# A transformer with local attention on one Trainium2 core: one of four rotations per tile moved ahead of its squares, and the sum of those squares moved behind the first average

## The chip, the cores and the metric

The kernel runs on one core of a Trainium2 chip. The metric is the device time of one execution in microseconds; lower is better. A core has five engines that work beside each other, each through its own list of instructions in order: TensorE (PE; its weight loads are shown as PEld), VectorE (DVE), ScalarE (ACT), GpSimd (POOL) and SyncE (SP, which issues transfers). An instruction starts when the one ahead of it on its engine lets it and the semaphores that it waits for have been raised.

## The reference

The model is a chain of four blocks on x of shape (4, 512, 128); each block is a cross attention to a context of 77 rows and then a feed-forward part, which is a mixture of 8 experts in blocks 0 and 3, and a quantised network with a depthwise convolution in block 1. In block 2 it is a local transformer of six layers, and the change lies there:

```python
def attn_layer(x, Wqkv, qs, ksc, Wo):
    qkv = x @ Wqkv
    q, k, v = split into 16 heads of 64
    q = l2norm(q) * qs
    k = l2norm(k) * ksc
    q = q * cos * scale + rotate_half(q) * sin * scale
    k = k * cos / scale + rotate_half(k) * sin / scale
    out = local_attention(q, k, v)      # windows of 32, each sees itself and the one before
    return out @ Wo
for i in range(6):
    x = attn_layer(shift_tokens(x), ...) + x
    x = ffn_layer(shift_tokens(x), ...) + x    # layernorm, W1, a * gelu(gate), W2
```

`l2norm` divides each head's 64 numbers by the root of the sum of their squares. That sum is what the change moves.

## The kernel before, in words

All other blocks are scheduled by a planner (`Plan`); the local transformer is not. In `local_transformer` the order of the work is written out by hand in one loop (L2027), under a manual schedule: every engine gets its instructions in the order in which the loop's body names them.

The activations stay on the chip: `Y[b]` holds a sequence of 512 tokens, features on partitions. The work is cut into tiles of 128 tokens: 6 layers x 4 sequences x 4 tiles = 96. One pass of the loop (a slot) works on three tiles at once: tile T is projected, rotated and normalised; tile T1, one behind, has its queries and keys turned to features on partitions and its scores and softmax computed; tile T2, two behind, has its averages, its output projection and its residual. Beside them a feed-forward F of one sequence runs over four slots, called phases 0 to 3 (n - 6 modulo 4): layernorm moments, norm and turning in phase 0, gate in 1 and 2, up in 2 and 3, down in 3. So 90 of the 96 slots with a tile T have one phase of a feed-forward too.

The steps that the change and the prediction touch:

- `queries_or_keys(T, kind, c)` (L1767): one matmul (L1774, it runs as two passes) gives 512 columns, that is 8 heads, of queries (kind 0) or keys (kind 1), c = 0 or 1, into `ps_mm`, a ring of two PSUM banks; ScalarE squares them into `sq` (L1776), a ring of two buffers.
- `rotate(T, kind, c)` (L1779): VectorE multiplies the bank by a table into `rc` (L1784, ring of six), then the halves swapped by another table into `rs` (L1787, ring of two), then sums `sq` over each head into `ss` (L1796); GpSimd adds `rs` to `rc` (L1797).
- `normalise(T)` (L1800): once all four sums are there, VectorE (L1807, L1808) and GpSimd (L1812 to L1815) find the inverse roots and GpSimd scales the four `rc` (L1818).
- `probabilities(T2)` (L1901): TensorE transposes P (L582), ScalarE copies it to `PT` in two halves (L1904).
- `average(T2, g)` and `normalised(T2, g)` (L1906, L1921): 64 small matmuls (L1914) into the bank pair `av`, then VectorE's reciprocal (L1923) and product (L1924).
- `scores(T1)` and `softmax(T1)` (L1866, L1889): the scores go into a bank pair `sc`, of which there is one; VectorE takes the maximum (L1893) and subtracts it into `P` (L1894); ScalarE's exponential follows (L1899).
- `ff_stage`: its matmuls (L1951, L1961, L1972, L1983, L1995) take the same pair `sc`; VectorE's part is L510 to L522 and L1711 in phase 0 and L1986 in phase 3; GpSimd finds a root (L514, L515) between L512 and L522.

On VectorE a slot reads, in order: first rotation of queries with its sum, [statistics in phase 0, or a product of the feed-forward in phase 3], reciprocal and product of the first average, [norm in phase 0], second rotation with its sum, reciprocal and product of the second average, two rotations of keys with their sums, L1807, L1808, maximum, subtraction, residual (L1945).

The ring of two in PSUM means that the third projection of a tile can start only when the bank of the first has been read by both ScalarE and VectorE. The framework makes the second reader of a bank wait for the first one: before the change, L1784 waits for L1776.

Of the kernel before, what the change touches and what calls it, by code (L numbers as in the profile page):

```python
# [25 lines left out]
ALU = mybir.AluOpType  # L26
AX = mybir.AxisListType
# [94 lines left out]
def bc(ap, shape, *axes):  # L122

    for a in axes:
        ap = ap.unsqueeze(a)
    return ap.to_broadcast(shape)
# [112 lines left out]
def tile_kernel(ctx: ExitStack, tc: tile.TileContext, A: dict, out: bass.AP):  # L239
    nc = tc.nc  # L240
    V, G, SC, PE, DMA = nc.vector, nc.gpsimd, nc.scalar, nc.tensor, nc.sync
# [40 lines left out]
    def p_mm(*shape):  # L282
        return psum(shape, "mm", 2)

    def p_tr(*shape):
        return psum(shape, "tr", 2)
# [54 lines left out]
    for b in range(B):  # L341
        t = xpool.tile([128, NT, D], F32, name=f"x{b}", tag=f"x{b}")
# [26 lines left out]
    with banks(), tc.tile_pool(name="prep", bufs=1) as prep:  # L369
# [26 lines left out]
        t = p_tr(128, B, SK)  # L396
# [3 lines left out]
        t = p_tr(128, 4, D)  # L400
# [3 lines left out]
        t = p_tr(128, 8)  # L404
# [3 lines left out]
        t = p_tr(128, 2, E)  # L408
# [1281 lines left out]
    def local_transformer(Y):  # L1690
        with ExitStack() as es:
# [28 lines left out]
            def load(i):  # L1720


                W = A["L2_ffn_Wqkv"][i]
                w = []
                for j in range(4):
                    t = wp.tile([128, 512], F32, name="wqk", bufs=8)
                    DMA.dma_start(t, W[:, 512 * j : 512 * j + 512])
                    w.append(t)
                wv = wp.tile([128, 2, 512], F32, name="wv")
                for x0 in range(2):  # L1730
                    DMA.dma_start(
                        wv[:, x0].rearrange("p (k d) -> p k d", d=LD),
                        W[:, 2 * INNER :].rearrange("p (k x d) -> p x k d", x=2, d=LD)[:, x0],
                    )
                wo = wp.tile([128, 8, D], F32, name="wo")
                DMA.dma_start(wo, A["L2_ffn_Wo"][i].rearrange("(c p) d -> p c d", p=128))
                w1 = wp.tile([128, 2 * DI], F32, name="lw1")
                DMA.dma_start(w1, A["L2_ffn_W1"][i])
                w2 = wp.tile([128, 3, D], F32, name="lw2")
                DMA.dma_start(  # L1740
                    w2[:, 0:2], A["L2_ffn_W2"][i][0:256].rearrange("(c p) d -> p c d", p=128)
                )
                DMA.dma_start(w2[: CH_W[2], 2], A["L2_ffn_W2"][i][256:DI])
                qs = wp.tile([128, 2, LD], F32, name="qs")
                DMA.dma_start(qs[:, 0], A["L2_ffn_q_scale"][i].partition_broadcast(128))
                DMA.dma_start(qs[:, 1], A["L2_ffn_k_scale"][i].partition_broadcast(128))
                return w, wv, wo, w1, w2, qs
# [19 lines left out]
            def queries_or_keys(T, kind, c):  # L1767

                b, tt = T.b, T.tt
                if T.ss is None:  # L1770
                    T.ss = small.tile([128, 2, LH], F32, name="ss")
                lhs = Y[b][:, 128 * tt : 128 * tt + 128]
                t = p_mm(128, 8, LD)
                PE.matmul(t, lhs, T.w[2 * kind + c], start=True, stop=True)  # L1774
                sq = tp.tile([128, 8, LD], F32, name="sq")
                SC.activation(sq, t, AF.Square)  # L1776
                T.raw[kind, c] = t, sq

            def rotate(T, kind, c):  # L1779

                tt = T.tt
                t, sq = T.raw.pop((kind, c))
                a = tp.tile([128, 8, LD], F32, name="rc", bufs=6)
                V.tensor_tensor(a, t, bc(T.tabs[:, 2 * kind, tt], [128, 8, LD], 1), ALU.mult)  # L1784

                r = tp.tile([128, 8, LD], F32, name="rs")
                V.tensor_tensor(  # L1787
                    r.rearrange("p h (x d) -> p h x d", x=2),
                    t.rearrange("p h (x d) -> p h x d", x=2)[:, :, ::-1],
                    bc(  # L1790
                        T.tabs[:, 2 * kind + 1, tt].rearrange("p (x d) -> p x d", x=2),
                        [128, 8, 2, LD // 2], 1,
                    ),
                    ALU.mult,
                )
                V.tensor_reduce(T.ss[:, kind, 8 * c : 8 * c + 8], sq, AX.X, ALU.add)  # L1796
                G.tensor_tensor(a, a, r, ALU.add)  # L1797
                T.rot[kind, c] = a

            def normalise(T):  # L1800


                n = 2 * LH
                ss = T.ss.rearrange("p a b -> p (a b)")
                y = small.tile([128, n], F32, name="rn_y")
                t = small.tile([128, n], F32, name="rn_t")
                V.tensor_scalar(ss, ss, 1e-24, -0.5, ALU.max, ALU.mult)  # L1807
                V.tensor_scalar(  # L1808
                    y.bitcast(I32), ss.bitcast(I32), -0.5, 0x5F3759DF - 0x40400000, ALU.mult, ALU.add
                )  # L1810
                for _ in range(3):
                    G.tensor_tensor(t, y, y, ALU.mult)  # L1812
                    G.tensor_tensor(t, t, ss, ALU.mult)
                    G.tensor_scalar(t, t, 1.5, None, ALU.add)
                    G.tensor_tensor(y, y, t, ALU.mult)  # L1815
                for (kind, c), a in sorted(T.rot.items()):
                    o = LH * kind + 8 * c
                    G.tensor_tensor(a, a, bc(y[:, o : o + 8], [128, 8, LD], 2), ALU.mult)  # L1818
# [135 lines left out]
            def ff_norm(F):  # L1954
                F.xn = lnp.tile([128, NT, D], F32, name="xn")
                layernorm(F.xn, F.t, F.found)
# [70 lines left out]
            for n in range(len(tiles) + 10):  # L2027
                T = tiles[n] if n < len(tiles) else None
                T1 = tiles[n - 1] if 0 <= n - 1 < len(tiles) else None
                T2 = tiles[n - 2] if 0 <= n - 2 < len(tiles) else None  # L2030
                m, phase = divmod(n - 6, 4)
                F = rows[m] if 0 <= m < len(rows) else None
                if T:
                    if n % 16 == 7 and T.i + 1 < DEPTH:
                        loaded[T.i + 1] = load(T.i + 1)
                    if n == 4:
                        fill, send, send_back = clear(lnp, 1)
                        fill(G)
                        send(DMA)
                        send_back(DMA)  # L2040
                    if n % 16 == 15 and T.i + 1 < DEPTH:
                        tabs[T.i + 1] = tables(loaded[T.i + 1][5])
                    T.before = tiles[n - 1] if T.tt else None
                    T.w, T.wv, T.wo = loaded[T.i][:3]
                    T.tabs = tabs[T.i]
                    queries_or_keys(T, 0, 0)
                if T2:
                    probabilities(T2)
                if T:
                    queries_or_keys(T, 0, 1)  # L2050
                    rotate(T, 0, 0)
                if F:
                    ff_stage(F, phase, False)
                if T2:
                    average(T2, 0)
                if T1:
                    turned(T1, 0)
                if T:
                    queries_or_keys(T, 1, 0)
                if T2:  # L2060
                    normalised(T2, 0)
                if F and phase == 0:
                    ff_norm(F)
                if T:
                    rotate(T, 0, 1)
                if T2:
                    average(T2, 1)
                if T1:
                    turned(T1, 1)
                if T:  # L2070
                    queries_or_keys(T, 1, 1)
                if T2:
                    normalised(T2, 1)
                if T:
                    rotate(T, 1, 0)
                if T2:
                    attended(T2)
                if T and T.tt == NT - 1 and n + 1 < len(tiles):
                    swap(tiles[n + 1].b)
                if T1:  # L2080
                    scores(T1)
                if T:
                    rotate(T, 1, 1)
                if T:
                    normalise(T)
                if T1:
                    softmax(T1)
                if T2:
                    project_out(T2)
                    residual(T2)  # L2090
                if T:
                    values(T, 0)
                    values(T, 1)
                if F:
                    ff_stage(F, phase, True)

            for b in range(B):
                for r, o in ((slice(0, 64), 0), (slice(64, 128), 1)):
                    t = p_tr(128, NT, 64)
# [38 lines left out]
```

## Time and profile before

| | |
|---|---|
| median of three runs | 2546.58 us (2539.14 to 2553.28) |
| the profiled execution | 2546.81 us, of which 2545.0 us span |
| granted TensorE clock, mean | 0.955 |
| busy: TensorE, VectorE, ScalarE, GpSimd | 89%, 70%, 48%, 60% of the span |
| busy in 1000 to 1400 us, inside the local transformer | TensorE 379.46, VectorE 322.16, ScalarE 222.35, GpSimd 302.30 of 400 us |
| first and last projection of the local transformer (L1774) | 519.2 and 2213.5 us |
| VectorE's softmax subtraction (L1894) | 96 times, 1.225 us each |

The local transformer is two thirds of the span. Its slots repeat so closely that one can lay them on top of each other: from one subtraction L1894 to the next it is at the median 20.15 us in a phase 0 slot, 15.65 in phase 1, 17.54 in phase 2 and 17.12 in phase 3, each taken from end to end. A row of a timeline has the start of an instruction, its duration, its engine and line, what it writes and reads, and in brackets how long its engine was idle before it and what ended that. A duration on VectorE is longer than the distance to the next start, since the end of one instruction overlaps the start of the next: two rotations that follow each other take 0.68 us each and start 0.60 us apart.

### The profile page before, as it was taken

The page shows a single profiled execution, that of the slowest core. Times are in us where ns is not written, and L with a number is a line of the kernel's source. Part 1 is how long each engine was busy: PE and PEld are TensorE (multiplying, and loading weights), DVE is VectorE, ACT ScalarE, POOL GpSimd, SP SyncE. Part 2 cuts the span into 40 slices and gives each one's busy share as a digit, 9 for nine tenths or more (in the row PEclk, how much of TensorE's full clock was granted, in tenths as well). Part 3 has the DMA queues.
Part 4 walks back from the last instruction along what each step waited for, and adds up shares of the span by engine and source line. Part 5 has one row for each costly group of instructions (what it writes and reads, how often), then busy time and mean ns, then how long its engine had stood idle before and what let it go on. Part 6 is the DMA issues. An engine that isn't in the chain of part 4 may idle for free.

```text
span 2545.0 us, 87636 instructions
## 1 busy us (share of the span) xinstructions
PE 2275.1 (89%) x37341; PEld 1472.7 (58%) x37341; DVE 1792.1 (70%) x4016; ACT 1228.5 (48%) x2161; POOL 1538.1 (60%) x2613
## 2 busy tenths in 40 slices
PE   7969799968999999999999999999999999978776
PEld 3547444536666666666666666666666666644455
DVE  5543475757787787878778787887878778737522
ACT  3622144534555555555555555555555555514322
POOL 2333303367777777777777777777777777702543
PEclk9979789989999999999999999999999999978888
DMA  6201200026211120101201121111211111011023
GB/s 165 81 27 39 67 1 2 1 58 138 72 30 34 28 77 26 34 26 34 77 25 34 28 76 34 26 32 28 77 31 29 34 28 34 26 36 49 27 67 89
DMA packets 134304, 116.20 MB, mean 46 GB/s; under 512 B 29505, under 2 KB 102700, under 8 KB 133916
## 3 DMA queue, kind: packets, MB, share of 16 engines
q1 hardware_dynamic: 128373, 102.81, 15.5%
q0 software_dynamic: 4608, 7.35, 0.9%
q8 instruction: 296, 4.85, 0.8%
q14 instruction: 92, 0.75, 0.1%
q10 hardware_dynamic: 935, 0.43, 0.1%
HBM read 42.84 MB, written 21.52 MB: 25 GB/s over the span
## 4 chain that ended last, share of the span: by engine, by line
PE 48%; DVE 31%; issue 6%; ACT 6%; POOL 6%; DMA 2%; SPq 0%; ACTq 0%; POOLq 0%; DVEq 0%
PE ps_mm L1774 6%; PE ps_tr L582 6%; DVE rc L1784 5%; DVE rs L1787 5%; DVE ss L1796 5%; PE ps_av L1938 3%; PE ps_sc L1983 3%; PE ps_tr L1853 3%; PE ps_av L1914 3%; PE ps_sc L1995 3%; DVE P L1894 2%; PE ps_sc L1883 2%; DVE la_mx L1893 2%; DVE ss L1807 2%; PE ps L1312 2%
## 5 line engine op out<-in xcount | busy, mean ns | idle before, releaser
L1797 POOL TENSOR_TENSOR rc<-rc,rs 128x512 f32<-128x512 f32 x384 | 488.2, 1273 | 281.8 <-DVE rs L1787 256.9
L1774 PE MATMUL ps_mm<-wqk,y 128*128 128x512 f32 x768 | 400.1, 604 | 35.3 <-DVE rs L1787 32.1
L1784 DVE TENSOR_TENSOR rc<-ps_mm,tabs 128x512 f32<-128x512 f32 x384 | 262.5, 684 | 204.0 <-ACT sq L1776 189.1
L1818 POOL TENSOR_TENSOR rc<-rc,rn_y 128x512 f32<-128x512 f32 x384 | 388.3, 1042 | 7.5
L1776 ACT ACTIVATE sq<-ps_mm 128x512 f32<-128x512 f32 x384 | 231.8, 604 | 177.1 <-PE ps_mm L1774 134.9
L1899 ACT ACTIVATE P<-P 128x1024 f32<-128x1024 f32 x96 | 101.5, 1057 | 435.5 <-DVE P L1894 435.5
L1787 DVE TENSOR_TENSOR rs<-ps_mm,tabs 128x512 f32<-128x512 f32 x384 | 261.6, 681 | 5.0 <-POOL rc L1797 4.7
L1796 DVE TENSOR_REDUCE ss<-sq 128x8 f32<-128x512 f32 x384 | 259.6, 676 | 0.0
L1914 PEld LDWEIGHTS ps_av<-v,PT 64*32 64x32 f32 x12288 | 140.5, 105 | 139.2 <-PE ps_tr L582 71.6
L582 PE MATMUL ps_tr<-cst,rc 128*128 128x128 f32 x1536 | 211.5, 281 | 9.8 <-POOL rc L1818 5.7
L1938 PE MATMUL ps_av<-aT,wo 128*128 128x128 f32 x1536 | 198.3, 282 | 3.5 <-issue 3.4
L1938 PEld LDWEIGHTS ps_av<-aT,wo 128*128 128x128 f32 x1536 | 179.2, 191 | 13.2 <-issue 4.6
L582 PEld LDWEIGHTS ps_tr<-cst,rc 128*128 128x128 f32 x1536 | 166.0, 141 | 29.6 <-POOL rc L1818 6.8
L1914 PE MATMUL ps_av<-v,PT 64*32 64x65 f32 x12288 | 172.6, 225 | 4.4 <-DVE attn L1924 1.1
L1774 PEld LDWEIGHTS ps_mm<-wqk,y 128*128 128x128 f32 x768 | 122.9, 193 | 80.1 <-DVE rs L1787 41.1
L1883 PE MATMUL ps_sc<-kT,qT 64*32 64x64 f32 x12288 | 145.8, 225 | 25.2 <-issue 18.4
L1017 POOL DMA_INDIRECT back<-ye,to x80 | 77.4, 968 | 141.8 <-DVE ye L1131 102.2
L1883 PEld LDWEIGHTS ps_sc<-kT,qT 64*32 64x32 f32 x12288 | 140.3, 105 | 34.9 <-issue 21.5
L1830 ACT COPY qT<-ps_tr 128x512 f32<-128x512 f32 x192 | 103.2, 589 | 91.7 <-PE ps_tr L582 89.4
L763 ACT ACTIVATE P<-ps,deltaT 77x512 f32<-77x512 f32 x192 | 115.0, 682 | 63.3 <-PE ps L757 63.2
L1830 ACT COPY kT<-ps_tr 128x512 f32<-128x512 f32 x192 | 103.2, 589 | 81.3 <-PE ps_tr L582 80.0
L1924 DVE TENSOR_TENSOR attn<-ps_av,la_den 128x512 f32<-128x512 f32 x192 | 132.8, 691 | 6.6
(391 smaller groups left out, 4449.4 us busy)
## 6 DMA issues: line engine op xcount, KB each, us to landing
v<-v SPq DMA_DIRECT2D x432, 65.0 KB
v<-v SPq DMA_DIRECT2D x96, 195.0 KB
wqk<-in_L_ffn_Wqkv_dram SPq DMA_DIRECT2D x24, 256.0 KB
sent<-xn SPq DMA_DIRECT2D x2, 2210.0 KB
xe<-sent SPq DMA_DIRECT2D x16, 260.0 KB
back<-xn SPq DMA_DIRECT2D x2, 2048.0 KB
raw<-in_L_ffn_W_dram SPq DMA_DIRECT2D x8, 512.0 KB
yb<-back SPq DMA_DIRECT2D x16, 256.0 KB
```

The source lines that it names most:

```text
L582: PE.transpose(t[:, i], src[:, i], ident)
L1774: PE.matmul(t, lhs, T.w[2 * kind + c], start=True, stop=True)
L1776: SC.activation(sq, t, AF.Square)
L1784: V.tensor_tensor(a, t, bc(T.tabs[:, 2 * kind, tt], [128, 8, LD], 1), ALU.mult)
L1787: V.tensor_tensor(r.rearrange("p h (x d) -> p h x d", x=2), t.rearrange("p h (x d) -> p h x d", x=2)[:, :, ::-1], bc(T.tabs[:, 2 * kind + ...
L1796: V.tensor_reduce(T.ss[:, kind, 8 * c : 8 * c + 8], sq, AX.X, ALU.add)
L1797: G.tensor_tensor(a, a, r, ALU.add)
L1818: G.tensor_tensor(a, a, bc(y[:, o : o + 8], [128, 8, LD], 2), ALU.mult)
L1830: SC.copy(t[:, 4 * c : 4 * c + 4, lead:], to_features(T.rot[kind, c].rearrange("p (k x) d -> p k (x d)", x=2)),)
L1883: PE.matmul(T.banks[32 * w : 32 * w + 32, z, k], T.qT[r, k, 32 * w : 32 * w + 32], T.kT[r, k, 32 * w : 32 * w + 64], start=False, stop=Tru ...
L1914: PE.matmul(T.means[32 * w : 32 * w + 32, x0, k], T.PT[r, 4 * g + k, 32 * w : 32 * w + 32], (T.v1 if w % 2 else T.v2)[r, x0, 4 * g + k], s ...
L1938: PE.matmul(t, T.wo[:, c], T.aT[:, c], start=(c == 0), stop=(c == 7))
```

## The change

The square of the first half of the queries (kind 0, c 0) is taken out of `queries_or_keys`, and its sum out of `rotate`. In the slot, the first rotation now comes ahead of that square and right behind the first projection's matmul and the copies of P's transposes; the second projection follows. The sum comes behind the reciprocal and product of the first average (in phase 0 behind the norm too), just ahead of the second rotation. So VectorE is the first reader of that bank, and ScalarE waits for it. The other three quarters of a tile keep their order.

```diff
                 PE.matmul(t, lhs, T.w[2 * kind + c], start=True, stop=True)
+                T.raw[kind, c] = [t, None]
+                if kind or c:
+                    squares(T, kind, c)
+
+            def squares(T, kind, c):
+                t = T.raw[kind, c][0]
                 sq = tp.tile([128, 8, LD], F32, name="sq")
                 SC.activation(sq, t, AF.Square)
-                T.raw[kind, c] = t, sq
+                T.raw[kind, c][1] = sq
 
             def rotate(T, kind, c):
...
-                V.tensor_reduce(T.ss[:, kind, 8 * c : 8 * c + 8], sq, AX.X, ALU.add)
                 G.tensor_tensor(a, a, r, ALU.add)
                 T.rot[kind, c] = a
+                if kind or c:
+                    summed(T, kind, c)
+
+            def summed(T, kind, c):
+                sq = T.raw.pop((kind, c))[1]
+                V.tensor_reduce(T.ss[:, kind, 8 * c : 8 * c + 8], sq, AX.X, ALU.add)
...
                 if T2:
                     probabilities(T2)
                 if T:
+                    rotate(T, 0, 0)
+                    squares(T, 0, 0)
                     queries_or_keys(T, 0, 1)
-                    rotate(T, 0, 0)
                 if F:
                     ff_stage(F, phase, False)
...
                 if F and phase == 0:
                     ff_norm(F)
                 if T:
+                    summed(T, 0, 0)
                     rotate(T, 0, 1)
```

In the changed kernel L1776, L1784, L1787, L1796, L1894, L1914, L1923 and L1986 are L1782, L1790, L1793, L1809, L1905, L1925, L1934 and L1997.

More of the change, by code (lines that the diff above doesn't have):

```diff
@@ L1774, in queries_or_keys @@
                 PE.matmul(t, lhs, T.w[2 * kind + c], start=True, stop=True)
+                T.raw[kind, c] = [t, None]
[3 more added lines that the diff above has]
+                t = T.raw[kind, c][0]
                 sq = tp.tile([128, 8, LD], F32, name="sq")
                 SC.activation(sq, t, AF.Square)
-                T.raw[kind, c] = t, sq
+                T.raw[kind, c][1] = sq
             def rotate(T, kind, c):
                 tt = T.tt
-                t, sq = T.raw.pop((kind, c))
+                t = T.raw[kind, c][0]
                 a = tp.tile([128, 8, LD], F32, name="rc", bufs=6)
```

## The prediction

> **What bounds the kernel now.** The page's first lines name TensorE (89% busy), but its groups show the wait that this change goes for: VectorE idle for 189.1 us before L1784 until ScalarE's squares were done, and L1796, the sum that is moved, 384 x 0.68 us with no idle time before it.
>
> ```profile
> PE 2275.1 (89%) x37341; PEld 1472.7 (58%) x37341; DVE 1792.1 (70%) x4016; ACT 1228.5 (48%) x2161; POOL 1538.1 (60%) x2613
> ...
> L1784 DVE TENSOR_TENSOR rc<-ps_mm,tabs 128x512 f32<-128x512 f32 x384 | 262.5, 684 | 204.0 <-ACT sq L1776 189.1
> ...
> L1796 DVE TENSOR_REDUCE ss<-sq 128x8 f32<-128x512 f32 x384 | 259.6, 676 | 0.0
> ```
>
> A wait is worth only what ends behind it, so next I read the timeline, one slot (one pass of the loop at L2027) at a time. I count time in a slot from the end of the previous softmax subtraction P (L1894). First VectorE's timeline of a phase 3 slot, from 1527.33; columns: start, duration, instruction, and in brackets the idle time before it and what ended it.
>
> ```profile
> 1526.10 1.23 DVE L1894 TENSOR_TENSOR P<-ps_sc,la_mx 128x1024 f32<-128x1024 f32 x1
> ...
> 1531.02 0.69 DVE L1784 TENSOR_TENSOR rc<-ps_mm,tabs 128x512 f32<-128x512 f32 x1
> 1531.62 0.68 DVE L1787 TENSOR_TENSOR rs<-ps_mm,tabs 128x512 f32<-128x512 f32 x1
> 1532.22 0.68 DVE L1796 TENSOR_REDUCE ss<-sq 128x8 f32<-128x512 f32 x1
> 1532.92 0.75 DVE L1986 SCALAR_TENSOR_TENSOR fh<-ps_sc,cols,fh 85x512 f32<-85x512 f32 x1
> 1533.71 0.21 DVE L1923 RECIPROCAL la_den<-ps_av 128x8 f32<-128x8 f32 x1
> 1533.95 0.69 DVE L1924 TENSOR_TENSOR attn<-ps_av,la_den 128x512 f32<-128x512 f32 x1
> 1534.56 0.68 DVE L1784 TENSOR_TENSOR rc<-ps_mm,tabs 128x512 f32<-128x512 f32 x1
> ...
> 1543.38 1.23 DVE L1894 TENSOR_TENSOR P<-ps_sc,la_mx 128x1024 f32<-128x1024 f32 x1
> ```
>
> See two halves. From the second rotation (1534.56, call it rc01) VectorE works almost without a gap until P ends. Over all slots from 656 to 2230 us that stretch is at the median 9.75 us in phases 0, 1 and 2, with no idle time, and 9.85 us in phase 3. Starts lie 0.60 us apart, so one more reduction in this stretch costs 0.60. And what follows P? TensorE's timeline around the next slots:
>
> ```profile
> 1544.75 2.81 PE L1995 MATMUL ps_sc<-fh,lw 128*128 128x512 f32 x6 [0.29 <-DVE P L1894]
> 1547.40 1.02 PE L1774 MATMUL ps_mm<-wqk,y 128*128 128x512 f32 x2
> 1548.26 1.03 PE L582 MATMUL ps_tr<-cst,P 128*128 128x128 f32 x8
> 1549.13 1.02 PE L1774 MATMUL ps_mm<-wqk,y 128*128 128x512 f32 x2
> 1549.99 0.60 PE L1951 MATMUL ps_sc<-cst,y 128*128 128x128 f32 x4
> 1550.53 0.86 PE L1914 MATMUL ps_av<-v,PT 64*32 64x65 f32 x64
> ...
> 1564.76 0.63 PE L1961 MATMUL ps_sc<-cst,xn 128*128 128x128 f32 x4 [1.09 <-DVE P L1894]
> ```
>
> The feed-forward matmuls (L1995, L1961, L1972 or L1983) start 0.14 us after P, since they need its bank. Behind them, in order and without a gap, come the next projections, transposes and averages (L1914). So the loop that sets a slot is: P, TensorE to the end of the first average, VectorE to the next P. ScalarE's square in front of rc00 lies beside TensorE's part of it.
>
> **The change, part by part.** Nothing is added in number. It moves, per tile, one rotation (two instructions) ahead of the square, the square behind the copies of P's transposes (L1904), and one reduction (0.60 us) from ahead of the reciprocal L1923 to just ahead of rc01. L1923 waits for the average. So the reduction leaves a place where VectorE would wait anyway, and enters the full stretch. New rc01 = (start of L1923) + 0.84 (L1923 0.24, L1924 0.60) + 0.60; in phase 0 the normalisation L522 lies between as well.
>
> Phase 3: L1986 of 85 rows waits for its matmul, L1923 stays at 6.38 after P; rc01 moves from 7.23 to 7.82, +0.60. The small gaps after rc01 take back 0.00 to 0.31, as each slot has. In 11 of 22 slots TensorE itself reaches L1995 late, 0.32 to 0.86 after P would allow, and takes the rest. Slot by slot 0.60 less the gap less that lateness, not below 0, adds up to 5.8 us.
>
> Phase 0: rc00 at 4.54 waits for L1711 (the result's addition, to 4.51), so it gains 0.1. The statistics L510, at 6.34 behind the reduction, now wait for the transposes L1951 (end 5.98): 6.03. All to L522 follows 0.31 earlier (GpSimd's add is done at 7.15, the root L514 moves from 7.59 to 7.28). Then +0.60: rc01 +0.29. P's next reader had waited 1.09 already, in 21 of 22 slots there is no slack: 22 x 0.29 = 6.4 us (23 slots, one with slack). If each L510 starts on its own transpose it is +0.1; if nothing moves earlier, +0.6.
>
> Phase 1: ScalarE copies P's transposes ahead of the square. The average at 3.74 waits for the first copy; the projection before it is over by about 3.46, so it starts at 3.48 and ends at 4.36 instead of 4.74 (0.88 for 1.00). L1923 at 4.39 instead of 5.05, rc01 at 5.83 against 5.88: nothing, within -0.1 and +0.3 (average not earlier). I take 0, since L1972 follows P closely and a gain of 0.05 is soon used up.
>
> Phase 2: the wait of 4.65 us before rc00 goes (table load and gelu stand ahead of the square), but the average ends at 6.64 and L1923 starts at 6.94. The copies ahead of the square let the average end 0.1 to 0.15 earlier: L1923 at about 6.53, rc01 at 7.97 against 7.78, +0.2 (0.34 if the average stays). TensorE is late by 0.18 or more in 6 of 22 slots, so 16 x 0.2 = 3.1 us (one slot has a gap).
>
> Four slots without a feed-forward (start 556 to 600): average 573.46 to 574.32, L1923 574.35: +0.5 each, 2 us.
>
> Other queues: no DMA moves. The squares' ring has two buffers, so the third square now waits for the moved reduction. In phase 0 that is 10.55 instead of 8.75, and the keys' copies (L1830) end at 12.2 instead of 11.15; the transposes that need their bank come at 12.8. Cover 0.6 us; I cost it at 0. In the other phases the reduction is over (5.8 to 7.9) before the third square starts (6.7 to 8.8).
>
> Sum: 6.4 + 0 + 3.1 + 5.8 + 2 = 17 us. The profiled execution took 2546.81 us (span 2545.0), practically the median 2546.58: **2564 us**.
>
> The Trainium skill, page "Perfetto Trace Analysis", § Identifying Performance Opportunities, Optimization Strategy, says to look for the gaps on the engine to be improved, find what they wait for, and let that start sooner. By it the 189.1 us before L1784 are the gap to close, and the sum would be up to 2546.8 - 189 = 2358 us. The rows of L1923 above speak against it: the gap closes, and the wait moves to L1923.
>
> **The rivals.**
> *TensorE alone sets the slot* (ends not slower). For it: TensorE is busy for 379.5 of the 400 us from 1000 to 1400, and is the later one at L1995 in 11 of 22 slots. Then the moved 0.60 costs nothing, and the averages' earlier start is left: 0.26 x 23 + 0.15 x 22 = 9 us, 2538 us. It decides where TensorE is late at P by over 0.6 us in most slots; the trace has that in 6 of 22 in phase 3, in 3 of 22 each in phases 1 and 2 and in none in phase 0. Chance 0.12.
> *The gap closes to the end* (faster): if L1923 did not wait, rc01 would come earlier by the gap less the reduction, 1.1 us or so in phases 1 and 2: 2546.8 - 45 x 1.1 = 2497 us. It needs averages that end over 1 us earlier; TensorE's order forbids it. Chance 0.03.
> *TensorE's lateness moves away* (slower still): these late slots follow pauses in its own queue. Without them 0.29 x 23 + 0.5 x 22 + 0.3 x 22 + 2 = 26 us, 2573 us; if the third square's wait in phase 0 also comes through with 0.3, 7 us more, 2580. Chance 0.22.
> *Only half of it shows* (phase 0 at +0.1, phase 2 at 0.1): 2 + 1.5 + 5.8 + 1 = 10 us, 2557. Chance 0.13.
>
> **How the numbers follow.** My case, 2558 to 2570, has 0.50. With the small case and three quarters of the late case (to 2580) it makes 0.8, so the range is 2550 to 2580; what is left out is TensorE's case, the faster one and the far end of the late one. A measurement of this kernel can tell about 0.5% (12.7 us) from no change, so slower means over 2559.3: 0.67 (0.45 of mine, the late case); same 0.28 (the small case, 0.10 of TensorE's, 0.05 of mine); faster 0.05 (the rest).
>
> **What would show it.** After: no idle time on ScalarE's squares before L1790 (the old L1784) for the first rotation; instead an idle time ahead of L1934 (L1923) that waits for L1925 (the average), about 1.7 us in phase 1 and 2.4 us in phase 2, and 0.8 us ahead of the 85-row product L1997 (L1986) in phase 3; rc01 to P still 9.75; from P to rc01 longer by 0.3, 0, 0.2 and 0.6 in phases 0 to 3; matmuls waiting for P longer. It is wrong if L1934 shows no wait, or if P to rc01 is shorter in phases 1 and 2.

## The result and the profile after

The changed kernel took 2569.65 us at the median of seven runs (2562.88 to 2571.98), the one before 2548.35 us (2539.14 to 2554.03) beside it: a ratio of 1.008, with a 95% interval of 1.0059 to 1.0100. It is slower by about 21 us; 17 were forecast, and the range was 2550 to 2580. The profiled execution of the change took 2569.88 us with a span of 2568.1, 23.1 more than before.

The page of the changed kernel, the groups of the rotation, the square and the sum (after the count: busy us and mean ns, then the idle time before the group and what ended most of it):

```profile
L1790 DVE TENSOR_TENSOR rc<-ps_mm,tabs 128x512 f32<-128x512 f32 x384 | 262.2, 683 | 107.9 <-PE ps_mm L1774 88.2
...
L1782 ACT ACTIVATE sq<-ps_mm 128x512 f32<-128x512 f32 x384 | 221.0, 606 | 141.2 <-DVE ss L1809 52.9
...
L1809 DVE TENSOR_REDUCE ss<-sq 128x8 f32<-128x512 f32 x384 | 259.4, 675 | 1.4 <-ACT sq L1782 1.4
```

The change does what it says: ahead of the rotation VectorE hardly waits for ScalarE's squares any more (7.9 us, 189.1 before), and its idle time there is down from 204.0 to 107.9 us. Yet the kernel is slower. Here is VectorE's timeline of the changed kernel in a phase 3 slot, the one that answers to the slot of the prediction:

```profile
1540.83 1.22 DVE L1905 TENSOR_TENSOR P<-ps_sc,la_mx 128x1024 f32<-128x1024 f32 x1
...
1545.52 0.68 DVE L1790 TENSOR_TENSOR rc<-ps_mm,tabs 128x512 f32<-128x512 f32 x1
1546.12 0.68 DVE L1793 TENSOR_TENSOR rs<-ps_mm,tabs 128x512 f32<-128x512 f32 x1
1547.65 0.75 DVE L1997 SCALAR_TENSOR_TENSOR fh<-ps_sc,cols,fh 85x512 f32<-85x512 f32 x1 [0.84 <-PE ps_sc L1994]
1548.44 0.21 DVE L1934 RECIPROCAL la_den<-ps_av 128x8 f32<-128x8 f32 x1
1548.68 0.69 DVE L1935 TENSOR_TENSOR attn<-ps_av,la_den 128x512 f32<-128x512 f32 x1
1549.29 0.68 DVE L1809 TENSOR_REDUCE ss<-sq 128x8 f32<-128x512 f32 x1
1549.88 0.68 DVE L1790 TENSOR_TENSOR rc<-ps_mm,tabs 128x512 f32<-128x512 f32 x1
...
1558.41 1.23 DVE L1905 TENSOR_TENSOR P<-ps_sc,la_mx 128x1024 f32<-128x1024 f32 x1
```

See the 0.84 us of idle time ahead of the 85-row product, where the sum stood before, and the sum now between the average's product and the second rotation. From P's end (1542.05) the second rotation starts after 7.83 us; before the change it was 7.23 (1534.56 from 1527.33). From there to the end of P it is 9.76 us, without a gap.

What VectorE waited for in the local transformer, before the change and then after it (total us, times, longest):

```profile
DVE rc L1784 <- ACT sq L1776: 162.8, 44, 4.7
...
DVE fh L1986 <- PE ps_sc L1983: 38.7, 22, 2.4
...
DVE la_den L1923 <- PE ps_av L1914: 7.8, 4, 6.1
```

```profile
DVE rc L1790 <- PE ps_mm L1774: 83.8, 44, 3.3
DVE la_den L1934 <- PE ps_av L1925: 80.5, 43, 2.3
...
DVE fh L1997 <- PE ps_sc L1994: 55.9, 44, 2.3
```

The 162.8 us did not go: they became a wait for the projection, one for the first average (7.8 to 80.5) and one for the feed-forward's matmul (38.7 to 55.9). Of the 7.8 us, 6.1 are a single wait behind the last tile, which the second list ends ahead of; without it the average's wait grew from 1.7 to 80.5 us. And what TensorE waits for, before and after:

```profile
PE ps_sc L1961 <- DVE P L1894: 22.9, 21, 1.1
...
PE ps_sc L1983 <- DVE P L1894: 3.3, 12, 0.3
PE ps_sc L1972 <- DVE P L1894: 3.3, 13, 0.4
...
PE ps_sc L1995 <- DVE P L1894: 0.3, 1, 0.3
```

```profile
PE ps_sc L1972 <- DVE P L1905: 23.0, 21, 1.1
...
PE ps_sc L1994 <- DVE P L1905: 9.6, 16, 0.7
...
PE ps_sc L1983 <- DVE P L1905: 7.2, 13, 0.8
PE ps_sc L2006 <- DVE P L1905: 7.1, 12, 0.7
```

The four feed-forward matmuls that need P's bank waited 29.8 us for it, and now 46.9: 17 of the 23 us show at this gate (L1961, L1972, L1983 and L1995 are L1972, L1983, L1994 and L2006 after).

For a finer look, every slot was measured from one softmax subtraction's end to the next and added up by phase, over the same 86 slots of each kernel (22 of phase 0, 21 of phase 1, 21 of phase 2, 22 of phase 3; the first and last ones left out). Each row is one profiled execution.

| slots, us in sum | phase 0 | phase 1 | phase 2 | phase 3 | all | whole kernel over before |
|---|---|---|---|---|---|---|
| before | 446.8 | 335.0 | 369.1 | 379.2 | 1530 | 1 |
| the change | 451.7 | 335.1 | 375.2 | 388.2 | 1550 | 1.0080 (1.0059 to 1.0100) |
| e1 sum moved alone | 451.3 | 342.3 | 377.1 | 389.0 | 1560 | 1.0115 (1.0075 to 1.0155) |
| e2 rotation ahead alone | 440.1 | 330.9 | 366.2 | 386.6 | 1524 | 0.9972 (0.9945 to 0.9998) |
| e3 change, short sum | 443.3 | 328.9 | 366.1 | 380.9 | 1519 | 0.9961 (0.9935 to 0.9987) |
| e4 before, short sum | 441.9 | 334.0 | 367.9 | 379.0 | 1523 | 0.9968 (0.9950 to 0.9985) |
| e5 three square buffers | 452.1 | 336.1 | 375.1 | 389.0 | 1552 | 1.0077 (1.0050 to 1.0104) |
| e6 order by phase | 442.9 | 332.9 | 366.5 | 380.4 | 1523 | 0.9957 (0.9937 to 0.9976) |
| e7 change in phase 3 alone | 445.5 | 338.4 | 369.3 | 389.8 | 1543 | 1.0059 (1.0037 to 1.0082) |
| e8 new order in phase 0 alone | 442.9 | 336.0 | 369.3 | 381.3 | 1530 | 0.9980 (0.9958 to 1.0002) |
| e9 split copies | 441.6 | 331.1 | 365.8 | 378.9 | 1517 | 0.9944 (0.9926 to 0.9963) |

Three remarks on reading it. The chips that ran e1 to e6 took longer for the kernel before (2603 to 2604 us) and that of e7 to e9 2555 us, so each ratio is against the runs of before on its own chip. From 1000 to 2200 us, inside the local transformer, the granted clock is 1.00 in all these profiles, so the slots compare across chips. The change and e5, which should be alike, differ by 2 us in sum: at least so much is noise. And since a slot runs from P to P, a TensorE that reaches the feed-forward's matmul late after the P of phase 3 lengthens the row of phase 0, not that of phase 3; in the same way each phase passes its lateness to the next.

### The profile page after: what moved, and what is told of

Read it like the earlier page. It is cut to its first block, busy times and chain, and to the rows that moved or that the text cites. A ratio compares the mean times of both kernels' runs of the same rounds, so it can differ in the third digit from the quotient of the medians.

```text
span 2568.1 us, 87636 instructions
## 1 busy us (share of the span) xinstructions
PE 2268.5 (88%) x37341; PEld 1468.9 (57%) x37341; DVE 1793.5 (70%) x4016; ACT 1227.1 (48%) x2161; POOL 1540.9 (60%) x2613
## 3 DMA queue, kind: packets, MB, share of 16 engines
q8 instruction: 296, 4.85, 0.8%
## 4 chain that ended last, share of the span: by engine, by line
PE 50%; DVE 33%; issue 6%; POOL 6%; DMA 3%; ACT 2%; SPq 1%; POOLq 0%; ACTq 0%; DVEq 0%
PE ps_mm L1774 7%; DVE ss L1809 6%; PE ps_tr L582 6%; DVE rc L1790 5%; DVE rs L1793 5%; DVE P L1905 3%; PE ps_av L1925 3%; PE ps_sc L1983 3%; DVE la_mx L1904 3%; PE ps_sc L1994 3%; PE ps_sc L2006 2%; PE ps_av L1949 2%; DVE ss L1818 2%; PE ps_tr L1864 2%; DVE attn L1935 2%
## 5 line engine op out<-in xcount | busy, mean ns | idle before, releaser
L1790 DVE TENSOR_TENSOR rc<-ps_mm,tabs 128x512 f32<-128x512 f32 x384 | 262.2, 683 | 107.9 <-PE ps_mm L1774 88.2
L1782 ACT ACTIVATE sq<-ps_mm 128x512 f32<-128x512 f32 x384 | 221.0, 606 | 141.2 <-DVE ss L1809 52.9
L1793 DVE TENSOR_TENSOR rs<-ps_mm,tabs 128x512 f32<-128x512 f32 x384 | 261.4, 681 | 5.6 <-POOL rc L1802 5.4
L1809 DVE TENSOR_REDUCE ss<-sq 128x8 f32<-128x512 f32 x384 | 259.4, 675 | 1.4 <-ACT sq L1782 1.4
L1925 PEld LDWEIGHTS ps_av<-v,PT 64*32 64x32 f32 x12288 | 136.0, 105 | 133.8 <-PE ps_tr L582 71.6
L1894 PE MATMUL ps_sc<-kT,qT 64*32 64x64 f32 x12288 | 145.9, 225 | 32.7 <-issue 23.6
L1925 PE MATMUL ps_av<-v,PT 64*32 64x65 f32 x12288 | 167.5, 225 | 1.2 <-DVE attn L1935 1.1
L1894 PEld LDWEIGHTS ps_sc<-kT,qT 64*32 64x32 f32 x12288 | 140.1, 105 | 42.7 <-issue 26.7
L1915 ACT COPY PT<-ps_tr 128x512 f32<-128x512 f32 x192 | 103.3, 594 | 88.1 <-PE ps_tr L582 88.1
```

Source lines behind the costliest of these rows:

```text
L1793: V.tensor_tensor(r.rearrange("p h (x d) -> p h x d", x=2), t.rearrange("p h (x d) -> p h x d", x=2)[:, :, ::-1], bc(T.tabs[:, 2 * kind + ...
L1894: PE.matmul(T.banks[32 * w : 32 * w + 32, z, k], T.qT[r, k, 32 * w : 32 * w + 32], T.kT[r, k, 32 * w : 32 * w + 64], start=False, stop=Tru ...
L1925: PE.matmul(T.means[32 * w : 32 * w + 32, x0, k], T.PT[r, 4 * g + k, 32 * w : 32 * w + 32], (T.v1 if w % 2 else T.v2)[r, x0, 4 * g + k], s ...
```

## The experiments

The theory was that of the prediction: the moved sum leaves a place where VectorE waits for TensorE and enters the full stretch from the second rotation to P. The main rival: the cost comes from the square, which ScalarE now does second and later.

### e1: the sum moved, square and rotation as before

Edit against the changed kernel:

```diff
-                if kind or c:
-                    squares(T, kind, c)
+                squares(T, kind, c)
...
-                    rotate(T, 0, 0)
-                    squares(T, 0, 0)
                     queries_or_keys(T, 0, 1)
+                    rotate(T, 0, 0)
```

> Only the sum is moved; square and rotation stand as before the change. Theory (the moved sum leaves VectorE's wait for the average and enters its full stretch): as slow as the change or slower, since the copies for the average are not ahead of the square now: from P to the second rotation +0.34 in phases 1 and 2, +0.6 in phase 3, +0.25 in phase 0, some 30 us over before, about 2577 us. Rival (the cost is that ScalarE reads the bank second and squares later): the square is where it was, so 2547 to 2552 us.

Measured: 1.0115, slots 1560 us, 30 more than before. With the square in its old place the kernel is not rescued but slower still: the rival falls. The second rotation starts 0.35 and 0.34 us later in phases 1 and 2 (6.23 against 5.88, 8.12 against 7.78), 0.59 in phase 3. So the sum's new place costs 30 us of slots, and the new places of the rotation and its square give 10 of it back in the change.

### e2: the rotation ahead, the sum ahead of the first average's reciprocal

Edit against the changed kernel:

```diff
+                if T:
+                    summed(T, 0, 0)
                 if T2:
                     normalised(T2, 0)
                 if F and phase == 0:
                     ff_norm(F)
                 if T:
-                    summed(T, 0, 0)
                     rotate(T, 0, 1)
```

> Rotation ahead of the square as in the change, but the sum goes ahead of the reciprocal of the first average (in phase 0 behind the statistics, in phase 3 behind the 85-row product). Theory: the sum lies in the wait again in phases 0, 1 and 2, and rc01 comes earlier than before the change by 0.38, 0.2 and 0.2 us; in phase 3 there is no wait left behind the 85-row product, +0.5. Sum -8 -3 -3.5 +8 = about 7 us under before, 2541 us. Rival (the later square costs): still about 2565 to 2570 us.

Measured: 0.9972, slots 1524 us, 6 less than before and 26 less than the change. VectorE's timeline of e2 in a phase 2 slot:

```profile
1412.10 0.68 DVE L1793 TENSOR_TENSOR rs<-ps_mm,tabs 128x512 f32<-128x512 f32 x1
1414.63 0.69 DVE L1809 TENSOR_REDUCE ss<-sq 128x8 f32<-128x512 f32 x1 [1.85 <-ACT sq L1782]
1415.23 0.20 DVE L1934 RECIPROCAL la_den<-ps_av 128x8 f32<-128x8 f32 x1
1415.46 0.69 DVE L1935 TENSOR_TENSOR attn<-ps_av,la_den 128x512 f32<-128x512 f32 x1
1416.07 0.68 DVE L1790 TENSOR_TENSOR rc<-ps_mm,tabs 128x512 f32<-128x512 f32 x1
```

The sum waits 1.85 us for the square, but in the time that the average needs anyway: it ends and the reciprocal starts at once, 6.73 us after P at the median (6.94 before, 6.60 with the change and the sum still to do). Phases 0 to 2 gain 7, 4 and 3 us. In phase 3 the 85-row product stands ahead of the sum, nothing is left to wait for, and 7 us are lost. A wait ahead of an instruction says nothing by itself: the change closes the wait for the squares and is slower, e2 leaves 1.85 us of it in this slot and is faster.

### e3 and e4: the sum made short, in the change and before it

Edit of both, ahead of the reduction (only 4 of each head's 64 squares are added up in that quarter):

```diff
+                if not kind and not c:
+                    sq = sq[:, :, 0:4]
                 V.tensor_reduce(T.ss[:, kind, 8 * c : 8 * c + 8], sq, AX.X, ALU.add)
```

> The changed kernel, but the moved sum takes only 4 of each head's 64 squares (the other 60 of that quarter are left out). Theory: that instruction falls from 0.68 to about 0.1 us, so each slot loses about 0.5 us where VectorE sets it, up to where TensorE is next (0.2 in phase 1): 30 to 36 us less than the change, about 2534 us. Rival (the place of the square costs, not the sum's length): 2563 us or more.

> The kernel before, with the same short sum of 4 of 64 squares. Theory: before the change the sum lay mostly in a wait, so shortening it gives little: 0.31 us in phase 0 (the statistics then wait for the transposes), 0.2 in phases 1 and 2, nothing in phase 3 (the 85-row product waits for its matmul): some 15 us, 2532 us, and with that within 5 us of the change with the short sum. Rival: with the sum short in both, the change stays slower by about 20 us.

Measured: 0.9961 and 0.9968. With a short sum the two kernels are alike (slots 1519 and 1523 us), though they differ by 20 with the whole one: the difference hangs on the sum's length in its place. VectorE itself shows the same: the second rotation of e3 starts within 0.1 us of that of e4 in phases 0, 2 and 3 (0.24 us sooner in phase 1), so it is not only a common TensorE behind it that makes them alike. The row of e3's reduction (ns least, median, most):

```profile
L1811 DVE TENSOR_REDUCE ss<-sq x384: 173/675/681, 561.5 to 2241.5; 128x8 f32<-128x32 f32 x96, 128x8 f32<-128x512 f32 x96
```

It fell from 0.68 to 0.17 us, 0.50 per slot, 43 us over 86 slots; 31 of them came out in the change and 7 before it (15 were expected there). Before the change the sum was cheap, but what was hoped for in phases 1 and 2 did not all come: VectorE reached the second rotation 0.25 and 0.24 us sooner, and then the stretch to P grew from 9.75 to 9.90 us at the median in each. TensorE is next there.

### e5: three buffers for the squares

```diff
-                sq = tp.tile([128, 8, LD], F32, name="sq")
+                sq = tp.tile([128, 8, LD], F32, name="sq", bufs=3)
```

> The changed kernel with three buffers for the squares in place of two, so that the third square no longer waits for the moved sum (the profile of the change shows 52.9 us of ScalarE's idle time there). Theory: that wait had cover, since the keys' transposed banks are needed later; the time stays that of the change, 1.008 of before (within 0.2%), though the 52.9 us go from ScalarE. Rival (the squares' ring carries the cost): down by up to 2% to the time of before or under it.

Measured: 1.0077, the change's own ratio. What ScalarE waited for in the local transformer, with the change and then with e5:

```profile
ACT kT L1841 <- PE ps_tr L582: 56.9, 66, 1.1
ACT sq L1782 <- DVE ss L1809: 50.7, 22, 2.3
...
ACT sq L1782 <- PE ps_mm L1774: 31.7, 87, 0.8
```

```profile
ACT kT L1841 <- PE ps_tr L582: 77.4, 89, 1.5
ACT sq L1782 <- PE ps_mm L1774: 73.0, 174, 2.0
```

The wait of 2.3 us per phase 0 slot for the moved sum is gone, and about the same time is spent waiting for TensorE. It was covered, as the prediction had it.

### e6: the order chosen by phase

Edit against e2: in phase 3 the square, the rotation and the sum stay as before the change.

```diff
+                    T.early = F is not None and phase == 3
...
                 if T:
-                    rotate(T, 0, 0)
-                    squares(T, 0, 0)
+                    if not T.early:
+                        rotate(T, 0, 0)
+                        squares(T, 0, 0)
                     queries_or_keys(T, 0, 1)
+                    if T.early:
+                        rotate(T, 0, 0)
...
-                if T:
+                if T and not T.early:
                     summed(T, 0, 0)
```

> Rotation ahead of the square and sum ahead of the first average's reciprocal in phases 0, 1 and 2 and in the slots without a feed-forward; phase 3 wholly as before the change. Theory: the slots of phases 0 to 2 as in the run with the rotation ahead alone (440, 331 and 366 us in sum), those of phase 3 as before (379), so 1516 us against 1530 before: 14 us or 0.5% faster than before (ratio 0.9945), and 1.4% faster than the change. Rival (a phase 3 slot is slowed by what its neighbours do): phase 3 stays above 384 us and the ratio at 0.997 or more.

Measured: 0.9957; clearly faster than before, but of the 14 us expected in the slots 7 came. Phase 3 gave its 6 us over e2 (380.4 for 386.6), and phases 0 and 1 took 5 of them back. What TensorE waited for in e6:

```profile
PE ps_sc L1894 <- issue: 29.8, 24, 1.8
...
PE ps_sc L1972 <- DVE P L1905: 14.2, 13, 1.1
```

The wait for P behind phase 0 has fallen (23.0 with the change), and TensorE's own pauses among the scores, which wait for no semaphore that the profile shows, have grown to 29.8 us (15.1 before). With P earlier, TensorE is the later one: the feed-forward's matmul behind phase 3 starts 0.45 us after P at the median (0.31 before, 0.22 in e2; 0.15 where TensorE is not late). Over all slots this matmul starts 7.5 us later after P than before the change, in sum, and the stretch from the second rotation to P takes 3.2 us more. The rival that neighbours slow phase 3 is not what happened; an earlier P is in part lost to a late TensorE.

### e7 and e8: one phase alone

e7 has the change's order in phase 3 and the old one elsewhere. Edit against the changed kernel:

```diff
+                    T.early = not (F is not None and phase == 3)
...
                 if T:
-                    rotate(T, 0, 0)
-                    squares(T, 0, 0)
+                    if not T.early:
+                        rotate(T, 0, 0)
+                        squares(T, 0, 0)
                     queries_or_keys(T, 0, 1)
+                    if T.early:
+                        rotate(T, 0, 0)
...
-                if T:
+                if T and not T.early:
                     summed(T, 0, 0)
+                if T:
                     rotate(T, 0, 1)
```

e8 has e2's order in phase 0 alone. Edit against e6:

```diff
-                    T.early = F is not None and phase == 3
+                    T.early = not (F is not None and phase == 0)
```

> The change in phase 3 slots alone; all other slots as before the change. Question: how much of +0.60 per slot comes through where TensorE had been late half of the time. If a late TensorE stays as late as it was (the prediction's count), the phase 3 slots add up to 385 us (379.2 + 5.8). If its lateness is a debt from pauses that longer slots let it work off, 388 us or more, as in the whole change; all other phases within 2 us of before. Ratio 1.002 to 1.004.

> Rotation ahead and sum ahead of the first average's reciprocal in phase 0 slots alone; all other slots as before the change. Theory (the price of each phase is its own place of the sum): phase 0 slots 440 us in sum against 446.8, the others within 2 us of before, ratio 0.997. Rival (a slot gives its gain to TensorE's lateness in the next one): phase 1 slots rise by 3 us or more.

Measured: e7 1.0059, above the 1.002 to 1.004 expected; its phase 3 slots add up to 389.8 us, 10.6 more than before. The expectation's two numbers, 385 and 388, set this row against a lateness that falls into the next one. Read with it, phases 3 and 0 together are 9.2 us longer, where counting the lateness as fixed gave 5.8: the late TensorE took 1.5 us, not 4.6, so the larger number was the nearer one. Phase 1 is also 3.4 us over before, where 2 was allowed; its slots are as before at the median (15.69 against 15.65), and 3.0 us of it sit in two of them, where TensorE reached the feed-forward's matmul 2.3 and 2.4 us late. e8: phase 0 is 3.9 us shorter (440 us in sum was expected, 442.9 came), the others are 3.3 us longer together, and the ratio of 0.998 has an interval that takes in 1. From the first projection to the second rotation a phase 0 slot is 0.25 us shorter (7.21 for 7.47), 5.5 us in sum, but the projection itself starts 0.11 later after P (3.04 for 2.92), since TensorE is late. The rival of e8 asked for 3 us or more in phase 1; 0.9 came there and 2.1 in phase 3. So its number did not come, and 3 us are hardly more than the noise, but what it says of the gain, that a late TensorE takes it, is seen ahead of the projection.

### e9: the square between the two halves of the copies

Edit against e6, for phases 1 and 2:

```diff
-                    probabilities(T2)
+                    probabilities(T2, *((0,) if split else (0, 1)))
...
                         squares(T, 0, 0)
+                    if split:
+                        probabilities(T2, 1)
                     queries_or_keys(T, 0, 1)
```

> The order chosen by phase (rotation ahead and sum ahead of the average's reciprocal in phases 0 to 2, phase 3 as before), and in phases 1 and 2 the square lies between the two halves of the copies of P's transposes. VectorE alone would gain: second rotation from 5.67 to 5.29 in phase 1 and from 7.57 to 7.44 in phase 2, 11 us less than by phase alone. If TensorE is the bound by now, the time from the second rotation to P grows by as much (idle time in it), and the sum of the slots stays within 3 us of 1523.

Measured: 0.9944 (0.9926 to 0.9963), the fastest of all, slots 1517 us, 5 less than e6: between the two cases. VectorE's waits in e9:

```profile
DVE ss L1809 <- ACT sq L1782: 44.3, 44, 1.4
...
DVE la_den L1935 <- PE ps_av L1926: 15.7, 26, 6.1
```

The sum waits 44.3 us for the square and the reciprocal only 15.7 for the average, 6.1 of them behind the last tile (80.5 with the change, ahead of it). The second rotation is where it should be, 5.31 and 7.45 us after P in phases 1 and 2, and the stretch behind it takes 9.84 and 9.90 us: TensorE takes part of the gain, not all. Its lead over e6 lies within the intervals of the two.

## Why the prediction was right, step by step

*The loop.* P, TensorE to the first average, VectorE to the next P: held. The stretch from the second rotation to P is 9.75 us in all phases after the change too, and in e1 to e3 it stays at 9.75 to 9.81, so that they move with the start of the second rotation. In e4, phases 1 and 2, it does not stay (9.90): there TensorE is next.

*The moved wait.* Forecast ahead of L1934 were 1.7 us in phase 1, 2.4 in phase 2 and 0.8 ahead of the 85-row product; measured medians are 1.49, 2.32 and 0.85.

*Phase 0, +0.29 and 6.4 us.* A little too small: from the first projection's end to the second rotation it is 0.35 us longer, 7.7 us in sum. The slots show +0.22 and 4.9 us, since 2.8 us come off ahead of that: the feed-forward's matmul, and the projection behind it, start 0.13 us sooner after P on average. That is the lateness which the prediction counts under phase 3.

*Phase 1, nothing.* Measured +0.1 us; the average starts at 3.55 (3.48 forecast), the second rotation at 5.89 (5.83 forecast, 5.88 before).

*Phase 2, +0.2 and 3.1 us.* Mis-sized: the second rotation moved by 0.26, and the slots are 6.1 us longer. The average did not start earlier (5.70, as before); only its 0.94 us became 0.87. The lateness behind phase 2, which the forecast had take 1.3 us, took 1.6; it stands in the slots of phase 3.

*Phase 3, +0.60 and 5.8 us.* The second rotation moved by 0.59, 13.2 us in sum from the feed-forward's matmul on, and the small gaps behind it took back 2.7, as the prediction's slot-by-slot count has it. Mis-sized is the term "TensorE itself reaches L1995 late, 0.32 to 0.86 after P would allow, and takes the rest". By the rows of the kernel before, it should have taken 4.6 us; it took 2.8: the mean start of L1995 after P fell from 0.48 to only 0.35 us. (The 9.0 us of the table's phase 3 row are no measure of this, since the lateness stands in phase 0.) Nine of the 11 late slots are those where TensorE paused among the scores: before the change it went on 13.86 to 14.69 us after P, with the change 14.12 to 14.93, the pauses themselves 0.57 to 1.38 and 0.86 to 1.56 us. Since the pause ended later, part of the slack was not there. e7 shows the same with the change in phase 3 alone. What the pauses go with is told in the last section; why they ended later here was not found.

*The slots without a feed-forward, 2 us.* Measured +0.5, +0.3, +0.3 and +0.1, 1.3 us in sum. The first slot with one took 19.92 for 18.17 us, which had not been counted.

*The squares' ring, 0.* Held (e5).

*The rivals.* TensorE alone sets the slot: no, but it takes about half of the gain in e6 and, within the noise, most of it in e8. The gap closes to the end: no. TensorE's lateness moves away (2573): this has come true in part, behind phase 3. With it (1.7 us), the shifts of phases 0 and 2 (1.3 and 1.2) and the first slot with a feed-forward (1.8) make up most of the 6 us by which the profiled span lies above the forecast's 17; the medians of the runs lie 4 above it.

The Trainium skill, page "Perfetto Trace Analysis", § Identifying Performance Opportunities, Optimization Strategy, says to find the gaps of the engine one wants to improve and let what blocks it start sooner. This case adds that the gap has to be followed to what stands behind it: 162.8 us of gap were closed, and 80.5 us opened at the average that was late all the time. e2 and e9 use the rule the other way round: they leave a gap and put work in it.

## What to carry to other kernels

Before moving an instruction out of a wait, ask what the engine does with the time: if its next instruction waits for the same late thing, the time is free and something should stay in it. Measure each stretch from one gate to the next, see which has no idle time, and keep work out of that one, slot by slot, since the best place can differ between phases (e2 lost in phase 3 what it won in phase 0). And slack of another engine that comes from its pauses is no fixed sum: it grows or shrinks when the rest moves.

## What was not expected of the hardware

TensorE pauses in some runs of 128 small score matmuls, in nearly every second phase 3 slot and in some others, waiting for no semaphore that the profile shows; in phase 3 for 0.57 to 1.56 us. The place wanders regularly: before the change, in successive such slots, the pause comes behind 110, 112, 114 and so on to 126 of the 128 matmuls, with the change behind 112 to 126. All such pauses among the scores, in the slots with a feed-forward, add up to 15.1 us before the change, 17.8 with it and 29.8 in e6, whose list for TensorE has the same matmuls in the same order. One of them, before the change:

```profile
1183.90 0.41 PE L1874 MATMUL ps_sc<-maskw,identb 64*32 64x512 bf16 x8
1184.13 1.36 PE L1883 MATMUL ps_sc<-kT,qT 64*32 64x64 f32 x116
1186.06 0.33 PE L1883 MATMUL ps_sc<-kT,qT 64*32 64x64 f32 x12 [0.57 <-issue]
```

The traces' transfer records show what they go with. Queue q8, of the kind "instruction", moves 296 packets of 16384 bytes (4.85 MB on the page), one for every 256 of the 75805 records of TensorE in the trace before (matmuls, weight loads and those of its sequencer). In all eleven traces, from one pause of this kind to the next there is a multiple of 256 such records, give or take one, and each of the 331 pauses, also the fewer ones among the averages and the output projection, ends 1.21 to 1.71 us after a packet of this queue has landed; of all of TensorE's matmuls only 8% start at such a distance. The packet of the pause above was under way from 1183.78 to 1184.78 us. So these are, as far as timing can tell, waits of TensorE for its next instructions. The 128 score matmuls with their weight loads are 256 records and run in 1.46 us, where the packets of these slots take 0.88 to 1.93 us each, and the 1.2 us or more behind them come on top. No run here changes how the instructions arrive, and why a packet starts when it does is open.
